# Three 64-column matmuls become one of 192 columns in the way back to edges of a graph layer

## The chip, the core and the metric

The kernel runs on one core of a Trainium2 chip. TensorE (PE) multiplies matrices and writes into PSUM, VectorE (DVE) and ScalarE (ACT) work element by element, GpSimd (POOL) here issues the gathers of rows from memory, and SyncE (SP) issues plain transfers. [...] The metric is the device time of one execution in microseconds (us). Three runs of the kernel before took 2152.33, 2159.18 and 2159.98 us; the median, 2159.18 us, is the time before.

## The reference

One layer of a graph network on 6250 nodes of 64 features and 206250 edges, the edges sorted by their target:

```python
def _L0_gnn_ref(x, edge_index, edge_attr, W1, b1, W2, b2):
    src = edge_index[0]
    dst = edge_index[1]
    msg = jax.nn.relu(x[src] + edge_attr)
    agg = jax.ops.segment_sum(msg, dst, num_segments=x.shape[0])
    h = x + agg
    h = jax.nn.relu(h @ W1 + b1)
    return h @ W2 + b2
...
h = jnp.maximum(_layernorm(x, axis=-1), 0.0)
x = x + _L0_gnn_ref(h, edge_index, edge_attr_64, L0_gnn_W1, L0_gnn_b1, L0_gnn_W2, L0_gnn_b2)
```

For every edge a row of the normed nodes is fetched (`x[src]`), the edge's attributes are added, a Relu is taken, and the messages are summed by target.

## The kernel before

**Groups and steps.** The edges are worked in 268 groups of 768 (`GE`), and a last part: 128 partitions times 6 columns (`G`), 64 features each. The function `half(g)` is one step of the main loop, for groups 5 to 268, so 264 steps. The order of all instructions is the order in which the program is written; the framework only places the semaphores, and each engine goes through its own instructions as fast as its waits allow.

**Two ways to fetch a row.** Of the 6 columns of a group the first three are gathered by POOL with indirect transfers, one for each column (`gather`, L175). The last three (`H` = 3) are fetched by TensorE with one-hot matrices, and this is the way that the change touches. The normed rows lie in SBUF as three bf16 parts side by side (`hp`, 3 x 64 = 192 columns), whose sum is the fp32 row. Two groups make a set `k`.

- `find` (VectorE, L394) compares node numbers and gives `found`, one-hot columns.
- `slots_of` (TensorE, L417) multiplies `found` with `hp`: 16 matmuls of 192 columns with 32 weights each for one u, two u to a PSUM tile `half`. `slots_out` (ScalarE, L425) casts a tile to bf16 in `picked`. In a step two such tiles come first, and two or one later.
- `back` (VectorE, L403) makes the one-hot matrices `backs`, 128x128, seven (`Q`) for each of the three columns.
- `pick(g, cols)` (TensorE, L434) takes the picked rows back to their edges: for each column u, each of 7 q and each of the 3 parts t one matmul of 64 columns, all 21 of a column accumulated into the same 64 columns of PSUM. A group has 63 such matmuls. Its result is the PSUM tile `pick`, of which there are two.

**What a step does, by engine.** TensorE in `half(g)`: the sum of the last group's messages by target, `window_sum(g-1)` (12 matmuls, L492); the first two tiles of `slots_of`; `pick(g+1, (0, 1))`; the later tiles of `slots_of`; `pick(g+1, (2,))`; in some steps matmuls for ranks and sources (L238, L240, L267, L279) and the dense layers (L509, L520). VectorE: `sum_into_z(g-2)` (L458) adds an older group's window to `z`; `messages(g)` adds gathered rows to the attributes `ea` (L478), and the picked ones (L480); then `one_hot` (L464), `back`, `find` and ranks. ScalarE: the casts of the first two tiles, the Relu of `messages(g)` (L482), the casts of the later tiles. POOL runs ahead: a gather waits only for a free buffer (`edge`, 12 of them), which VectorE's work on an older group sets free. SP loads attributes 9 groups ahead (`AHEAD`).

**PSUM.** [...] `rows` and `half` have two each; `pick` has two tiles; the windows of four groups (`AB` = 4) share a tile `agg`, and there are two of these. `window_sum(g-1)` comes before `sum_into_z(g-2)` in the program.

The lines around which the rest turns, in `half` and in `messages`:

```python
messages(g)
if g < NG:
    pick(g + 1, (0, 1))
...
nc.vector.tensor_tensor(ea[:, lo:m], ea[:, lo:m], xg[:, lo:m], ALU.add)
if m < G:
    nc.vector.tensor_tensor(ea[:, m:], ea[:, m:], picks.pop(g), ALU.add)
```

Of the kernel before, what the change touches and what calls it, by code (L numbers as in the profile page):

```python
# [9 lines left out]
F32 = mybir.dt.float32  # L10
# [5 lines left out]
ALU = mybir.AluOpType  # L16
AX = mybir.AxisListType
DVE = mybir.EngineType.DVE

N, E, D = 6250, 206250, 64  # L20
P = 128
G = 6
# [10 lines left out]
W = 32  # L33
# [5 lines left out]
LOOK = 12  # L39
AHEAD = 9  # L40
LAG = 2
AB = 4
RV = 16

H = 3
# [7 lines left out]
Q = PARTS * S // P  # L53
XC = 14
RAW = 5
F0 = RAW
# [13 lines left out]
def kernel(  # L70
# [14 lines left out]
    nc = tc.nc  # L85
# [7 lines left out]
    psum = ctx.enter_context(tc.tile_pool(name="psum", bufs=2, space=bass.MemoryType.PSUM))  # L93
# [85 lines left out]
    def first_col(g):  # L179
        return 0 if g < NG else G - CT  # L180

    def pool_cols(g):
        return G - H if g >= F0 else G
# [195 lines left out]
    backs, sources, spots, found, picked, halves, picks = {}, {}, {}, {}, {}, {}, {}  # L379

    def source_load(k):
        sources[k] = rank.tile([P, PARTS * 2 * S], I16, name="sources")
        nc.sync.dma_start(out=sources[k][:PP], in_=lines[k // SETS][k % SETS].rearrange("(o m) s -> o (m s)", o=1)
                          .to_broadcast([PP, PARTS * 2 * S]))

    def spot_load(k):
        spots[k] = rank.tile([P, 2 * H * P], BF16, name="spots")
        nc.sync.dma_start(out=spots[k], in_=spot_rows[k * 2 * H:(k + 1) * 2 * H, :]
                          .rearrange("(o t) s -> o (t s)", o=1).to_broadcast([P, 2 * H * P]))
# [9 lines left out]
    def back(k, q0, q1):  # L399
        if q0 == 0:  # L400
            backs[k] = hot.tile([P, Q, 2 * H, P], BF16, name="backs")
        for q in range(q0, q1):
            nc.vector.tensor_scalar(backs[k][:, q].rearrange("p t s -> p (t s)"), spots[k].bitcast(I16),  # L403
                                    ids[:, q:q + 1], None, op0=ALU.is_equal)
        if q1 == Q:
            spots.pop(k)
# [3 lines left out]
    def slots_of(k, n0):  # L410
        ps = psum.tile([P, 2, 3 * D], F32, name="half", bufs=2)
        for u in range(2):
            i, q = divmod(n0 + u, Q)
            for b in range(BB):
                for j in range(J):
                    m = q * J + j
                    nc.tensor.matmul(ps[j * S:(j + 1) * S, u], found[k][:PP, b, m, i, :],  # L417
                                     hp[:, b * PARTS + m].rearrange("p t d -> p (t d)"),
                                     start=(b == 0), stop=(b == BB - 1))
        if n0 == 0:  # L420
            picked[k] = hot.tile([P, 2 * Q, 3 * D], BF16, name="picked")
        halves[k, n0] = ps

    def slots_out(k, n0):
        nc.scalar.copy(picked[k][:, n0:n0 + 2], halves.pop((k, n0)))  # L425

    def pick(g, cols):
        k, i = divmod(g - F0, 2)
        if cols[0] == 0:
            picks[g] = psum.tile([P, H, D], F32, name="pick", bufs=2)  # L430
        for u in cols:
            for q in range(Q):
                for t in range(3):
                    nc.tensor.matmul(picks[g][:, u], backs[k][:, q, i * H + u, :],  # L434
                                     picked[k][:, i * Q + q, t * D:(t + 1) * D],
                                     start=(q == 0 and t == 0), stop=(q == Q - 1 and t == 2))

    def norm_edges(xg):
        s = work.tile([P, G], F32, name="raw_s")
        nc.vector.tensor_reduce(s, xg, AX.X, ALU.add)  # L440
        nc.vector.tensor_scalar_mul(s, s, 1.0 / D)
        nc.vector.tensor_tensor(xg, xg, s.unsqueeze(2).to_broadcast([P, G, D]), ALU.subtract)
        sq = work.tile([P, G, D], F32, name="msg", bufs=3)
        nc.scalar.activation(sq, xg, AF.Square)
        fill()
        v = work.tile([P, G], F32, name="raw_v")
        nc.vector.tensor_reduce(v, sq, AX.X, ALU.add)
        nc.scalar.activation(v, v, AF.Sqrt, bias=eps_sb, scale=1.0 / D)
        fill()
        nc.vector.reciprocal(v, v)  # L450
        nc.vector.scalar_tensor_tensor(xg, xg, 0.0, v.unsqueeze(2).to_broadcast([P, G, D]),
                                       op0=ALU.max, op1=ALU.mult)

    aggs, hots, taken, msgs, banks = {}, {}, {}, {}, []

    def sum_into_z(g):
        at = window_start(g)
        nc.vector.tensor_tensor(z[:, ds(at, W)], z[:, ds(at, W)], aggs.pop(g), ALU.add)  # L458

    def one_hot(g):  # L460
        lo = first_col(g)
        n = G - lo
        oh = work.tile([P, G, W], F32, name="oh")
        nc.vector.tensor_tensor(  # L464
            oh[:, lo:], slot[:, cols_of(g)].unsqueeze(2).to_broadcast([P, n, W]),
            slots[:, :W].unsqueeze(1).to_broadcast([P, n, W]), ALU.is_equal)
        hots[g] = oh

    def enter(g):
        if g <= NG and g not in taken:  # L470
            taken[g] = loaded[g] if g < RAW else load(g)

    def messages(g):
        lo, m = first_col(g), pool_cols(g)
        ea, xg = taken.pop(g)
        if g < RAW:
            norm_edges(xg)
        nc.vector.tensor_tensor(ea[:, lo:m], ea[:, lo:m], xg[:, lo:m], ALU.add)  # L478
        if m < G:
            nc.vector.tensor_tensor(ea[:, m:], ea[:, m:], picks.pop(g), ALU.add)  # L480
        msg = work.tile([P, G, D], F32, name="msg", bufs=3)
        nc.scalar.activation(msg[:, lo:], ea[:, lo:], AF.Relu)  # L482
        msgs[g] = msg

    def window_sum(g):
        lo, oh, msg = first_col(g), hots.pop(g), msgs.pop(g)
        if g % AB == 0:
            banks.append(psum.tile([P, AB, W], F32, name="agg", bufs=2))
        pa = banks[-1][:, g % AB]
        for j in range(lo, G):  # L490
            i = (j - lo) % 2
            nc.tensor.matmul(pa[i * D:(i + 1) * D], msg[:, j, :], oh[:, j, :], start=(j < lo + 2), stop=(j >= G - 2))  # L492
        aggs[g] = pa
# [41 lines left out]
    def blocks_behind(g):  # L535
        for c in sorted(res):
            store(c, *res.pop(c))
        for c in sorted(hid):
            res[c] = result(c, *hid.pop(c))
        for c in range(NB):  # L540
            if READY[c] == g:
                hid[c] = hidden(c)

    def chunk(i, then):

        if i % (2 * SETS) == 0 and 0 <= i // (2 * SETS) < NCH:
            then(i // (2 * SETS))

    def is_set(k):
        return 0 <= k < KS  # L550

    def half(g):
        k, i = divmod(g - F0, 2)
        first = ((0, 2), (8, 10))[i]
        later = ((4, 6), (12,))[i]
        now = is_set(k + 1)
        enter(g + AHEAD)
        if i == 0:
            if is_set(k + 3):
                source_load(k + 3)  # L560
        elif is_set(k + 3):
            spot_load(k + 3)
        if g >= 1:
            window_sum(g - 1)
        if now:
            for n0 in first:
                slots_of(k + 1, n0)
                slots_out(k + 1, n0)
        if g >= LAG:
            sum_into_z(g - LAG)  # L570
            blocks_behind(g - LAG)
        messages(g)
        if g < NG:
            pick(g + 1, (0, 1))
        if now:
            for n0 in later:
                slots_of(k + 1, n0)
                slots_out(k + 1, n0)
        if g < NG:
            pick(g + 1, (2,))  # L580
        one_hot(g)
        if i == 0:
            if is_set(k + 1):
                back(k + 1, 4, Q)
            if is_set(k + 2):
                find(k + 2, 0)
        else:
            if is_set(k + 2):
                back(k + 2, 0, 4)
                find(k + 2, 1)  # L590
        at = g - F0
        chunk(at + 14, rank_at)
        chunk(at + 13, rank_count)
        chunk(at + 12, rank_of)
        chunk(at + 11, rank_marks)
        chunk(at + 11, rank_turn)
        chunk(at + 10, rank_holds)
        chunk(at + 10, rank_fits)
        chunk(at + 9, source)
        if g in CHECKS:  # L600
            find_left(CHECKS.index(g))
# [90 lines left out]
        slots_out(0, n0)  # L692
    source_load(2)
    spot_load(2)
    pick(F0, (0, 1, 2))
    find(1, 0)
    find(1, 1)
    back(1, 0, 4)
# [25 lines left out]
    with tc.If(any_left > 0):  # L724
        with tc.For_i(0, NG, 1) as i:
# [4 lines left out]
            ea = edge.tile([P, G, D], F32, name="ea")  # L730
# [5 lines left out]
        ea = edge.tile([P, G, D], F32, name="ea")  # L736
# [46 lines left out]
```

## Time and profile before

| | |
|---|---|
| median of three runs | 2159.18 us |
| the profiled execution | 2166.87 us, of which the span of its instructions 2165.2 us |
| busy, TensorE matmuls | 1587.4 us (73%), 35792 matmuls |
| busy, weight loads | 1246.3 us (58%), 35792 |
| busy, VectorE | 964.1 us (45%) |
| busy, ScalarE | 598.1 us (28%) |
| busy, POOL | 864.5 us (40%) |
| granted TensorE clock, mean | 0.81 |

How to read the rows. A group of instructions by line reads: line, engine, operation, output<-input, shapes, count | busy us, mean ns of one | idle time of the engine before them and what ended it. A row of the time line reads: start (us from the span's start), duration, engine, line, operation, and in brackets the idle time before it. A row of windows reads: from:to, length, then for PE, PEld (weight loads), VectorE, ScalarE and POOL the busy time with the number of instructions in brackets, then the granted clock (1.00 is full), the share of the DMA engines in use and GB/s. "issue" is idle time for which the profile shows no wait. Matmuls overlap, so the duration of one is not its price; the distance from one group's start to the next one's is. A few per cent of the matmul records can be missing.

### The profile page before, as it was taken

How to read it: one execution, taken by the hardware profiler on the slowest of the kernel's cores; microseconds unless marked ns; L12 is line 12 of the kernel's file. 1: busy time of each engine (PE TensorE's matmuls, PEld its weight loads, DVE VectorE, ACT ScalarE, POOL GpSimd, SP SyncE). 2: the span in 40 equal slices, each digit the busy share in tenths (PEclk: the TensorE clock that was granted, in tenths of full speed). 3: DMA queues.
4: the chain of work that ended last, by engine and by line, in shares of the span. 5: the costliest groups of instructions: out<-in, count | busy, mean ns of one | idle time of the engine just before them, and what ended most of it. 6: DMA issues, size and time to landing. Idle time of an engine off the chain costs nothing.

```text
span 2165.2 us, 79562 instructions
## 1 busy us (share of the span) xinstructions
PE 1587.4 (73%) x35792; PEld 1246.3 (58%) x35792; DVE 964.1 (45%) x2721; ACT 598.1 (28%) x1351; POOL 864.5 (40%) x834
## 2 busy tenths in 40 slices
PE   1147787787778777777787778778777777778788
PEld 0135565565556655665565666556665566556566
DVE  7074443444444344444344444444444444444445
ACT  1132222232223222223222223222222322223223
POOL 7514433434444344434433443344434434443330
PEclk9998887777878788878778778777778987888779
DMA  5113233223333233333322323232323322323321
GB/s 165 29 47 88 73 95 81 71 75 83 78 81 88 80 74 77 88 79 88 83 72 76 88 72 90 75 85 74 89 71 82 96 76 70 89 77 91 81 77 35
DMA packets 112983, 172.67 MB, mean 80 GB/s; under 512 B 29185, under 2 KB 83585, under 8 KB 112637
## 3 DMA queue, kind: packets, MB, share of 16 engines
q1 hardware_dynamic: 85534, 139.02, 21.8%
q0 software_dynamic: 26240, 26.92, 7.5%
q8 instruction: 282, 4.62, 0.9%
q10 hardware_dynamic: 864, 1.60, 0.2%
q14 instruction: 63, 0.52, 0.1%
HBM read 163.56 MB, written 3.88 MB: 77 GB/s over the span
## 4 chain that ended last, share of the span: by engine, by line
PE 71%; issue 21%; another core or an unknown queue 3%; DVE 2%; DMA 2%; ACT 0%; DVEq 0%; POOL 0%; SPq 0%; ACTq 0%
PE pick L434 34%; PE half L417 25%; PE agg L492 8%; DMA x_sb<-in_x_dram 1%; PE rows L279 1%; PE rows L509 1%; PE rows L240 1%; PE rows L238 1%; PE rows L520 1%; PE rows L267 0%; DVE backs L403 0%; ACT z L318 0%; DVE found L394 0%; DVE rest L325 0%
## 5 line engine op out<-in xcount | busy, mean ns | idle before, releaser
L175 POOL DMA_INDIRECT xg<-h_rows,src_sb x790 | 831.1, 1052 | 1227.2 <-DVE ea L480 907.1
L434 PE MATMUL pick<-picked,backs 128*128 128x64 bf16 x16632 | 773.6, 207 | 245.3 <-issue 239.0
L434 PEld LDWEIGHTS <-backs 128*128 128x128 bf16 x16632 | 650.9, 107 | 412.4 <-issue 401.7
L425 ACT CAST picked<-half 128x384 bf16<-128x384 f32 x924 | 420.6, 480 | 1380.6 <-PE half L417 888.9
L417 PE MATMUL half<-hp,found 112*32 112x192 bf16 x14784 | 595.2, 283 | 196.9 <-issue 186.6
L417 PEld LDWEIGHTS <-found 112*32 112x32 bf16 x14784 | 379.6, 109 | 304.0 <-issue 267.7
L458 DVE TENSOR_TENSOR z<-z,agg 128x32 f32 x269 | 49.9, 185 | 714.1 <-PE agg L492 694.0
L403 DVE TENSOR_SCALAR backs<-spots,ids 128x768 bf16<-128x768 int16 x924 | 327.7, 414 | 0.0
L480 DVE TENSOR_TENSOR ea<-ea,pick 128x192 f32<-128x192 f32 x264 | 92.2, 349 | 407.7 <-PE pick L434 380.8
L492 PE MATMUL agg<-oh,msg 128*64 128x32 f32 x3224 | 187.9, 256 | 10.6 <-issue 8.1
L492 PEld LDWEIGHTS agg<-oh,msg 128*64 128x64 f32 x3224 | 153.2, 172 | 44.1 <-issue 27.8
L394 DVE TENSOR_SCALAR found<-sources,nodes_of 112x1792 bf16<-112x1792 int16 x264 | 178.0, 675 | 0.1
L482 ACT ACTIVATE msg<-ea 128x384 f32<-128x384 f32 x269 | 142.7, 530 | 5.3 <-DVE ea L478 3.0
L464 DVE TENSOR_TENSOR oh<-slot,slots 128x192 f32<-128x192 int16 x269 | 94.4, 351 | 0.0
L478 DVE TENSOR_TENSOR ea<-ea,xg 128x192 f32<-128x192 f32 x264 | 93.6, 355 | 0.7
L317 PE MATMUL rows<-ident,x_sb 112*64 112x112 f32 x56 | 12.7, 394 | 49.9 <-issue 42.5
L238 PE MATMUL rows<-at,upper 128*128 128x504 bf16 x44 | 25.7, 585 | 22.8 <-DVE at L232 21.5
L317 PEld LDWEIGHTS rows<-ident,x_sb 112*64 112x64 f32 x56 | 7.7, 160 | 55.2 <-issue 45.9
L279 PE MATMUL rows<-holds,marks 128*28 128x32 bf16 x792 | 29.5, 185 | 11.3 <-DVE holds L257 5.9
L175 POOL DMA_INDIRECT xr<-in_x_dram,src_sb x30 | 31.1, 1035 | 10.6 <-issue 8.8
L279 PEld LDWEIGHTS <-marks 128*28 128x28 bf16 x792 | 24.2, 100 | 15.5 <-DVE holds L257 6.0
L257 DVE TENSOR_TENSOR holds<-rank_of,from 128x576 bf16<-128x576 f32 x44 | 32.9, 749 | 0.0
(94 smaller groups left out, 391.3 us busy)
## 6 DMA issues: line engine op xcount, KB each, us to landing
sources<-source_row SPq DMA_DIRECT2D x132, 392.0 KB
ea<-in_edge_attr_dram SPq DMA_DIRECT2D x268, 192.0 KB
spots<-spot_rows SPq DMA_DIRECT2D x132, 192.0 KB
xg<-h_rows,src_sb POOLq DMA_INDIRECT x790
h_rows<-x_sb SPq DMA_DIRECT2D x4, 392.0 KB
x_sb<-in_x_dram SPq DMA_DIRECT2D x4, 388.5 KB
xb<-in_x_dram SPq DMA_DIRECT2D x12, 128.0 KB
out_dram<-o SPq DMA_DIRECT2D x12, 128.0 KB
```

The costliest lines, as they stand in the source:

```text
L175: nc.gpsimd.indirect_dma_start(out=xg[:, j, :], out_offset=None, in_=rows[:, :], in_offset=bass.IndirectOffsetOnAxis(ap=idx[:, j:j + 1], a ...
L279: nc.tensor.matmul(ps[:, i], mk[:, i * H + t, :], oh[:, i * H + t, :], start=(t == 0), stop=(t == H - 1))
L394: nc.vector.tensor_scalar(found[k][:PP, b].rearrange("p m i s -> p (m i s)"), sources[k][:PP], nodes_of[:PP, b:b + 1], None, op0=ALU.is_equal)
L403: nc.vector.tensor_scalar(backs[k][:, q].rearrange("p t s -> p (t s)"), spots[k].bitcast(I16), ids[:, q:q + 1], None, op0=ALU.is_equal)
L417: nc.tensor.matmul(ps[j * S:(j + 1) * S, u], found[k][:PP, b, m, i, :], hp[:, b * PARTS + m].rearrange("p t d -> p (t d)"), start=(b == 0) ...
L425: nc.scalar.copy(picked[k][:, n0:n0 + 2], halves.pop((k, n0)))
L434: nc.tensor.matmul(picks[g][:, u], backs[k][:, q, i * H + u, :], picked[k][:, i * Q + q, t * D:(t + 1) * D], start=(q == 0 and t == 0), st ...
L464: nc.vector.tensor_tensor(oh[:, lo:], slot[:, cols_of(g)].unsqueeze(2).to_broadcast([P, n, W]), slots[:, :W].unsqueeze(1).to_broadcast([P, ...
L478: nc.vector.tensor_tensor(ea[:, lo:m], ea[:, lo:m], xg[:, lo:m], ALU.add)
L480: nc.vector.tensor_tensor(ea[:, m:], ea[:, m:], picks.pop(g), ALU.add)
L482: nc.scalar.activation(msg[:, lo:], ea[:, lo:], AF.Relu)
L492: nc.tensor.matmul(pa[i * D:(i + 1) * D], msg[:, j, :], oh[:, j, :], start=(j < lo + 2), stop=(j >= G - 2))
```

## The change

`pick` writes all three parts with one matmul: 192 columns of `picked` go into 192 columns of PSUM, and only the 7 q are accumulated. A group then has 21 matmuls in place of 63, and the sum over the parts is left to VectorE. A new function `room` takes two PSUM tiles for a group, of two columns and of one, each column with four parts of 64; ScalarE copies the edges' attributes into the fourth part. In `messages` VectorE sums the four parts with a `tensor_reduce` for each tile and writes the result over the attributes, in place of the addition at L480. `room(g + 1)` stands in `half` between `messages(g)` and `pick(g + 1, (0, 1))`. [...]

```diff
-AB = 4
+AB = 8
...
     def pick(g, cols):
         k, i = divmod(g - F0, 2)
-        if cols[0] == 0:
-            picks[g] = psum.tile([P, H, D], F32, name="pick", bufs=2)
+        ps, lo = picks[g][len(picks[g]) - 2 + (cols[0] > 0)]
         for u in cols:
             for q in range(Q):
-                for t in range(3):
-                    nc.tensor.matmul(picks[g][:, u], backs[k][:, q, i * H + u, :],
-                                     picked[k][:, i * Q + q, t * D:(t + 1) * D],
-                                     start=(q == 0 and t == 0), stop=(q == Q - 1 and t == 2))
+                nc.tensor.matmul(ps[:, u - lo, :3].rearrange("p t d -> p (t d)"), backs[k][:, q, i * H + u, :],
+                                 picked[k][:, i * Q + q], start=(q == 0), stop=(q == Q - 1))
+
+    def room(g):
+        ea, m = taken[g][0], G - H
+        picks[g] = []
+        for lo, n in ((0, 2), (2, 1)):
+            ps = psum.tile([P, 2, 4, D], F32, name="pick", bufs=3)
+            nc.scalar.copy(ps[:, :n, 3], ea[:, m + lo:m + lo + n])
+            picks[g].append((ps, lo))
...
-    aggs, hots, taken, msgs, banks = {}, {}, {}, {}, []
+    aggs, hots, taken, msgs = {}, {}, {}, {}
+    bank = psum.tile([P, AB, W], F32, name="agg", bufs=1)
...
         if m < G:
-            nc.vector.tensor_tensor(ea[:, m:], ea[:, m:], picks.pop(g), ALU.add)
+            for (ps, at), n in zip(picks.pop(g), (2, 1)):
+                nc.vector.tensor_reduce(ea[:, m + at:m + at + n], ps[:, :n].rearrange("p j t d -> p j d t"), AX.X, ALU.add)
...
     def window_sum(g):
         lo, oh, msg = first_col(g), hots.pop(g), msgs.pop(g)
-        if g % AB == 0:
-            banks.append(psum.tile([P, AB, W], F32, name="agg", bufs=2))
-        pa = banks[-1][:, g % AB]
+        pa = bank[:, g % AB]
...
         messages(g)
         if g < NG:
+            room(g + 1)
             pick(g + 1, (0, 1))
...
-    pick(F0, (0, 1, 2))
+    room(F0)
+    pick(F0, (0, 1))
+    pick(F0, (2,))
```

## The prediction

> **What bounds the kernel now.** I read the page's chain of waits first, then its groups by line, the time line of one step, and last the busy times in short windows. A "step" below is one call of `half`, one group of 768 edges.
>
> ```profile
> PE 71%; issue 21%; another core or an unknown queue 3%; DVE 2%; DMA 2%; ACT 0%; DVEq 0%; POOL 0%; SPq 0%; ACTq 0%
> PE pick L434 34%; PE half L417 25%; PE agg L492 8%; DMA x_sb<-in_x_dram 1%; PE rows L279 1%; PE rows L509 1%; PE rows L240 1%; PE rows L238 1%; PE rows L520 1%; PE rows L267 0%; DVE backs L403 0%; ACT z L318 0%; DVE found L394 0%; DVE rest L325 0%
> L434 PE MATMUL pick<-picked,backs 128*128 128x64 bf16 x16632 | 773.6, 207 | 245.3 <-issue 239.0
> 143.30:2155.70 2012.40, 1557.55 (x35499) 1226.92 (x35494) 888.84 (x2575) 565.41 (x1288) 795.94 (x754) 0.80 0.31 80
> ```
>
> TensorE sets the end: 71% work, 21% "issue", where it waits for no semaphore. The main loop (last row) is 2012.4 us for 264 steps, 7.62 us each, at a mean clock of 0.80. The issue time has a place. These are windows over three batches of gathers on POOL, each split where TensorE's first long gap begins; the counts in brackets after the first two busy times are its matmuls and weight loads.
>
> ```profile
> 1010.08:1011.44 1.36, 1.31 (x47) 1.05 (x43) 1.36 (x5) 0.70 (x2) 1.08 (x1) 1.00 0.04 12
> 1011.44:1018.02 6.58, 2.36 (x33) 1.35 (x34) 1.18 (x4) 0.00 (x0) 4.80 (x5) 0.84 0.14 25
> 1026.06:1027.46 1.40, 1.26 (x40) 1.15 (x41) 1.40 (x5) 0.99 (x3) 1.09 (x2) 1.00 0.06 15
> 1027.46:1030.39 2.93, 1.40 (x19) 0.55 (x18) 0.78 (x2) 0.00 (x0) 1.95 (x2) 0.85 0.46 80
> 1228.68:1231.06 2.38, 2.38 (x55) 2.07 (x48) 2.38 (x7) 1.35 (x3) 2.07 (x2) 0.53 0.09 14
> 1231.06:1235.89 4.83, 1.68 (x26) 0.83 (x22) 0.76 (x3) 0.00 (x0) 3.61 (x5) 0.84 0.16 30
> ```
>
> While POOL gathers, TensorE gets some 80 to 100 instructions, at either clock, and then only 10 to 13 per us (67 in 6.58 us, 37 in 2.93, 48 in 4.83) until shortly after the batch. I read this as a reserve that is used up while the supply nearly stops; the reserve is an inference from the equal counts. A batch of three holds this for 4.33 us (1.40 + 2.93) and lets 118 instructions pass. So the number of instructions counts, more than their columns.
>
> **The price of columns.** Windows from one group's start to the next one's, then a time line:
>
> ```profile
> 1053.21:1055.56 2.35, 2.35 (x46) 2.26 (x42) 0.68 (x2) 0.92 (x3) 0.00 (x0) 0.50 0.91 250
> 1024.01:1024.73 0.72, 0.72 (x25) 0.67 (x21) 0.00 (x0) 0.66 (x2) 0.00 (x0) 1.00 0.98 188
> 1009.59:1010.92 1.33, 1.33 (x46) 1.28 (x43) 1.33 (x6) 1.19 (x3) 0.84 (x1) 1.00 0.14 25
> 1023.24:1024.01 0.77, 0.77 (x35) 0.61 (x32) 0.00 (x0) 0.20 (x1) 0.00 (x0) 1.00 0.91 302
> ...
> 1019.10 0.86 PE L492 MATMUL agg<-oh,msg 128*64 128x32 f32 x12
> 1019.89 1.47 PE L417 MATMUL half<-hp,found 112*32 112x192 bf16 x32
> 1021.29 2.02 PE L434 MATMUL pick<-picked,backs 128*128 128x64 bf16 x42
> ```
>
> At full clock 42 matmuls of 64 columns take 1.33 us and 21 take 0.72: 29 ns each and 0.11 fixed. At half clock 2.35 us for 42 is 53 ns each. For a 192-column matmul against 128 weights there is no row; the ends are 83 ns (32 matmuls of 192 columns at L417, four side by side, 0.77 us less 0.11, over 8) and 3 x 29 = 87. I take 83, and at half clock 3 x 53 = 160. So one matmul for three saves hardly any streaming: pick of two columns goes from 1.33 to 14 x 0.083 + 0.11 = 1.27 us, of the third from 0.72 to 0.69; at half clock both stay (2.35, 1.23). What it removes is 42 matmuls and 42 weight loads of about 270 instructions a step.
>
> **The wait that it adds.** `room` puts ScalarE copies ahead of pick, into the same PSUM tile. Whether a matmul then waits, though its columns are others, I read from the sums:
>
> ```profile
> 1024.73 0.54 PE L492 MATMUL agg<-oh,msg 128*64 128x32 f32 x12
> 1025.20 0.84 PE L417 MATMUL half<-hp,found 112*32 112x192 bf16 x32
> 1025.32 0.19 DVE L458 TENSOR_TENSOR z<-z,agg 128x32 f32 x1 [3.56 <-PE agg L492]
> 1025.43 0.36 DVE L478 TENSOR_TENSOR ea<-ea,xg 128x192 f32<-128x192 f32 x1
> 1025.71 0.35 DVE L480 TENSOR_TENSOR ea<-ea,pick 128x192 f32<-128x192 f32 x1
> 1025.77 0.86 ACT L425 CAST picked<-half 128x384 bf16<-128x384 f32 x2 [1.10 <-PE half L417]
> 1025.97 0.35 DVE L464 TENSOR_TENSOR oh<-slot,slots 128x192 f32<-128x192 int16 x1
> 1026.06 1.08 POOL L175 DMA_INDIRECT xg<-h_rows,src_sb  x1 [8.58 <-DVE ea L480]
> 1026.52 0.54 ACT L482 ACTIVATE msg<-ea 128x384 f32<-128x384 f32 x1
> ...
> 1012.18 0.18 DVE L458 TENSOR_TENSOR z<-z,agg 128x32 f32 x1
> ```
>
> L458 reads the window of an older group, yet it starts 0.05 us after the matmuls of the newest window end (1025.27): two engines on different columns of one PSUM tile are put in order. In the step at 1012.18 it doesn't wait; there the two windows lie in different tiles. With one `bank` of eight, VectorE waits in every step. I take it that pick waits for its copy likewise. On ScalarE that copy stands behind two casts and the Relu, and the Relu behind VectorE's sums. [...]
>
> ```profile
> L440 DVE TENSOR_REDUCE raw_s<-xr 128x6 f32<-128x384 f32 x5 | 2.7, 547 | 0.1
> L289 DVE TENSOR_REDUCE ln_s<-x_sb 112x14 f32<-112x896 f32 x4 | 4.3, 1086 | 4.6 <-DMA x_sb<-in_x_dram 4.6
> L318 ACT COPY z<-rows 64x448 f32<-64x448 f32 x12 | 6.4, 542 | 49.2 <-remote 42.1 <-PE rows L616 4.2 <-PE rows L317 1.9
> L318 ACT COPY z<-rows 64x224 f32<-64x224 f32 x4 | 1.4, 357 | 9.4 <-remote 9.4
> ```
>
> A reduce costs 1.05 ns an element and 0.14 us (539 ns for 512 more), so 512 elements 0.68 us and 256 0.41, against 0.35 for L480. These read the four parts with a stride, which no row shows; the low end is these prices less a tenth, the high end twice them. A copy is 0.83 ns a column and 0.17 us: 0.28 and 0.23.
>
> From the window's end (1025.20 is zero) at full clock: first reduce 0.51, second 1.10 (an operation's successor starts 0.09 before its end), end 1.51; Relu 1.56; copy 2.00 to 2.28 (Relu 0.53, overlap 0.09); pick 2.32. It now starts at 0.77, so TensorE stands 1.55 us in each step. At half clock the casts hold the Relu until 1.88 (the second block ends at 1.40), pick starts at 2.65: 1.25 us. Queued behind pick on TensorE is the rest of the step. The second copy ends before pick's third column is due. VectorE's added 0.74 us a step (195 us in all) and ScalarE's 0.5 lie beside TensorE: they have 889 and 565 us of work in the loop's 2012; only what stands in this chain counts. POOL's gathers go by L478 or L480 (ends 1025.79, 1026.06; the batch at 1010.08 runs on into a second one before the next L480), so I leave their start at 0.86.
>
> **The sum for a step.** Full clock before: first block 0.77; the batch from 0.86 to 5.19 lets 118 instructions pass, pick's 81 and 37 of the later block's 48 (64 or 32); 0.14 for those left, 0.72, some 0.40 for ranks and dense layers (an estimate), 0.47 for the window: 6.9 us. Half clock: 0.54 us of the first block (25), pick's 84 and 14 of the later block pass by 5.19; 0.75 + 1.23 + 0.50 + 0.79 follow: 8.46. With full clock for 60% of the time, which gives 0.80: 1/(0.6/6.9 + 0.4/8.46) = 7.45, against 7.62 measured.
>
> After, full clock: 0.77 + 1.55 + 1.27 + 0.61 + 0.69 + 0.40 + 0.47 = 5.75; only some 105 instructions fall in the batch, fewer than the 118 it lets pass, so the starving is gone. Half clock: 1.40 + 1.25 + 2.35 + 1.08 + 1.23 + 0.50 + 0.79 = 8.60. The clock goes with how busy the window before was:
>
> ```profile
> 1009.04:1012.46 3.42, 2.71 (x72) 1.95 (x71) 3.12 (x11) 1.28 (x3) 2.08 (x2) 1.00 0.13 24
> 1012.46:1015.87 3.41, 1.09 (x20) 0.69 (x18) 0.16 (x1) 0.00 (x0) 2.50 (x4) 1.00 0.15 28
> 1015.87:1019.28 3.41, 1.27 (x24) 1.04 (x26) 0.32 (x2) 0.52 (x2) 1.31 (x2) 0.50 0.12 20
> 1026.11:1029.52 3.41, 2.11 (x50) 1.51 (x49) 2.13 (x6) 0.94 (x3) 2.80 (x3) 1.00 0.26 28
> 1029.52:1032.94 3.42, 3.04 (x36) 1.84 (x37) 0.00 (x0) 0.48 (x1) 0.20 (x1) 0.50 0.58 182
> ```
>
> A window busy for 2.71 of 3.42 us is followed by full clock, those with 1.09 and 2.11 by half. A window that holds the whole stall is busy for about 1.9, so I take half the time at each clock: 1/(0.5/5.75 + 0.5/8.60) = 6.89, 0.56 us less than 7.45. [...] Over 264 steps 0.56 us is 147 us: 2166.87 for the profiled execution (span 2165.2) becomes 2020; the median of the runs lies 8 lower, so 2012.
>
> **The rivals.**
> No reserve after the stall (slower): what passes in a batch doesn't wait in a buffer, so pick resumes in the starved stretch at 12.6 instructions per us. From 2.32 to 5.19 pass 36, the remaining 40 and the rest take 2.06: 7.25 at full clock, with 8.60 mixed 7.87, +0.42 a step: 2269. It decides where fewer than about 60 instructions pass at once after the wait. Against it stand the equal counts at both clocks.
> A dear reduce: at twice its price the stall grows by 1.0 us, 6.75 and 9.6 give 7.93: 2285. From 0.55 us more the change loses. For it: four elements to a sum, strided. Against it: VectorE's rows all go by elements.
> The clock drops further, to 30% at full: 7.49, no change, 2169. For it: stall and remaining gaps are apart, so more windows have one. Against it: the starving, which drops it now, shrinks.
> No wait for the copies, if the two are told apart by columns: no stall, starving late in the step, 5.5 and 7.35 at 60%: 6.12, which is 1808. Against it stands L458.
>
> **How the numbers follow.** Forecast 0.57, no reserve 0.14, dear reduce 0.10, lower clock 0.12, no wait 0.07. The forecast alone spans 1925 to 2100 (share of full clock 60% to 40%, cheap or slightly dearer reduces). Down to 1925 and up to 2250 some 0.79 lie inside, with the lower clock and the lower part of the slow cases. Runs differ by 0.35% (2152.33 to 2159.98), so within 0.5% counts as the same. Faster: forecast and no wait, 0.64, and 0.03 of the clock case; same 0.06; slower 0.14 + 0.10 + 0.03.
>
> **What would show it.** Right: TensorE idle before L434's successor by some 1.5 us a step, released by ScalarE's copy; "issue" time down by more than half; gathers in batches of three only; reduces at 0.68 and 0.41 us. Wrong: pick following its block without a gap; gaps of 0.7 us right behind the stall; reduces above 1 us; a loop clock under 0.7.

## The result: 1803 us, and the profile after

| | before | after |
|---|---|---|
| median of four runs each, same chip | 2159.58 us | 1803.39 us (1787.49 to 1814.54) |
| ratio | | 0.833, 95% interval 0.827 to 0.839 |
| profiled execution, of which span | 2166.87, 2165.2 us | 1814.54, 1812.8 us |
| mean granted clock over the span | 0.81 | 0.92 |
| TensorE matmuls | 35792 | 24704 |
| VectorE busy | 964.1 us | 1137.3 us |

The change saves 356 us; 147 were forecast, and 1803 lies below the predicted range. All numbers of this section are from the chip of this comparison; other chips behave differently, which is shown further down. The profiled execution after is the slowest of its four, at a mean clock of 0.92 where the other three show 0.93 to 0.94.

The page's chain of waits can't be read this time: for the changed kernel it breaks off after some per cent of the span. The waits of TensorE are the first view instead. The columns are: waiting engine and line, what ended the wait, total us, times, longest us.

```profile
PE pick L432 <- ACT pick L440: 380.6, 244, 4.1
PE pick L432 <- issue: 17.1, 41, 3.3
```

The wait for ScalarE's copy is there, 380.6 us or 1.44 us a step (over 264 steps; the shares of a few steps are booked elsewhere). "Issue" ahead of `pick` fell from 239.0 to 17.1 us. Next are the page's line of the clock in 40 slices and its groups; last the groups kept apart by shape.

```profile
PEclk9999998998989989998999899889898899999889
L432 PE MATMUL pick<-picked,backs 128*128 128x192 bf16 x5544 | 635.1, 268 | 427.2 <-ACT pick L440 380.6
L417 PE MATMUL half<-hp,found 112*32 112x192 bf16 x14784 | 438.0, 260 | 9.9 <-DVE found L394 5.3
```

```profile
L487 DVE TENSOR_REDUCE ea<-pick 128x128 f32<-128x512 f32 x264 | 180.5, 684 | 0.1
L487 DVE TENSOR_REDUCE ea<-pick 128x64 f32<-128x256 f32 x264 | 109.5, 415 | 0.0
L440 ACT COPY pick<-ea 128x128 f32<-128x128 f32 x264 | 69.0, 261 | 0.0
L440 ACT COPY pick<-ea 128x64 f32<-128x64 f32 x264 | 54.1, 205 | 0.0
```

At L417, where the kernel before lost 186.6 us to "issue", TensorE now idles for 9.9 us in all. The reduces and copies cost what was forecast (0.684 and 0.415 us against 0.68 and 0.41; 0.261 and 0.205 against 0.28 and 0.23).

One step at full clock in the time line:

```profile
1003.65 0.54 PE L497 MATMUL agg<-oh,msg 128*64 128x32 f32 x12
1004.12 0.84 PE L417 MATMUL half<-hp,found 112*32 112x192 bf16 x32
1004.24 0.19 DVE L464 TENSOR_TENSOR z<-z,agg 128x32 f32 x1 [3.63 <-PE agg L497]
1004.41 0.36 DVE L484 TENSOR_TENSOR ea<-ea,xg 128x192 f32<-128x192 f32 x1
1004.69 1.01 DVE L487 TENSOR_REDUCE ea<-pick 128x128 f32<-128x512 f32 x2
1005.04 0.95 POOL L175 DMA_INDIRECT xg<-h_rows,src_sb  x1 [3.62 <-DVE ea L484]
1005.74 0.52 ACT L489 ACTIVATE msg<-ea 128x384 f32<-128x384 f32 x1 [0.20 <-DVE ea L487]
1006.17 0.40 ACT L440 COPY pick<-ea 128x128 f32<-128x128 f32 x2
1006.48 1.31 PE L432 MATMUL pick<-picked,backs 128*128 128x192 bf16 x14 [1.52 <-ACT pick L440]
1007.73 0.84 PE L417 MATMUL half<-hp,found 112*32 112x192 bf16 x32
1008.50 0.75 PE L432 MATMUL pick<-picked,backs 128*128 128x192 bf16 x7
```

The chain runs window, sum into `z`, addition, reduces, Relu, copy, `pick`, as it was worked out. The gathers start at 1005.04, and TensorE stands until 1006.48; then 14, 32 and 7 matmuls follow without a gap while POOL still gathers. From 1006.48 to 1007.73 the 14 matmuls take 1.25 us. All batches of gathers but two after the first 200 us have three: 243 of 245. Before, 123 had three, 58 six and 2 nine, where gathers less than 0.6 us apart count as one batch.

The whole loop, from the first `pick` to the last, in the view of windows:

```profile
143.14:1802.59 1659.45, 1224.02 (x24406) 987.05 (x24406) 1061.26 (x2837) 648.65 (x1814) 828.51 (x754) 0.92 0.35 96
```

That is 6.29 us a step against 7.62, with the clock at 0.92 against 0.80. The records of the clock in these two loops hold two values only, 1 and 0.5; half clock ruled for 816 of 2012 us before (41%) and for 276 of 1659 us after (17%). Idle time moved from "issue" to the copy and hardly shrank: 455 us in the loop before, of which `pick` and `half` lost 425.6 to "issue", and 435 after. What fell is work at half clock: TensorE was busy there for 659 us before and 255 after, and at full clock for 899 and 969. Its busy time in the loop went from 1557.55 to 1224.02 us, though 21 matmuls of 192 columns stream as many columns as 63 of 64.

### The profile page after: what moved, and what is told of

Read it like the earlier page. It is cut to its first block, busy times and chain, and to the rows that moved or that the text cites. A ratio compares the mean times of both kernels' runs of the same rounds, so it can differ in the third digit from the quotient of the medians.

```text
span 1812.8 us, 57727 instructions
## 1 busy us (share of the span) xinstructions
PE 1254.3 (69%) x24704; PEld 1006.5 (56%) x24704; DVE 1137.3 (63%) x2985; ACT 682.1 (38%) x1879; POOL 897.7 (50%) x834
## 3 DMA queue, kind: packets, MB, share of 16 engines
q0 software_dynamic: 26240, 26.92, 8.0%
## 5 line engine op out<-in xcount | busy, mean ns | idle before, releaser
L175 POOL DMA_INDIRECT xg<-h_rows,src_sb x790 | 863.7, 1093 | 826.4 <-DVE ea L484 651.4
L432 PE MATMUL pick<-picked,backs 128*128 128x192 bf16 x5544 | 635.1, 268 | 427.2 <-ACT pick L440 380.6
L432 PEld LDWEIGHTS <-backs 128*128 128x128 bf16 x5544 | 510.9, 106 | 537.4 <-issue 523.9
L425 ACT CAST picked<-half 128x384 bf16<-128x384 f32 x924 | 410.9, 481 | 918.5 <-PE half L417 827.6
L417 PE MATMUL half<-hp,found 112*32 112x192 bf16 x14784 | 438.0, 260 | 9.9 <-DVE found L394 5.3
L417 PEld LDWEIGHTS <-found 112*32 112x32 bf16 x14784 | 308.4, 100 | 74.5 <-issue 52.5
L487 DVE TENSOR_REDUCE ea<-pick 128x128 f32<-128x512 f32 (+1 forms) x528 | 268.1, 549 | 0.1
L497 PE MATMUL agg<-oh,msg 128*64 128x32 f32 x3224 | 156.6, 230 | 4.7 <-DVE z L464 1.1
L497 PEld LDWEIGHTS agg<-oh,msg 128*64 128x64 f32 x3224 | 126.3, 141 | 45.1 <-issue 33.5
L440 ACT COPY pick<-ea 128x128 f32<-128x128 f32 (+1 forms) x528 | 105.7, 233 | 0.0
```

The source lines that it names most:

```text
L175: nc.gpsimd.indirect_dma_start(out=xg[:, j, :], out_offset=None, in_=rows[:, :], in_offset=bass.IndirectOffsetOnAxis(ap=idx[:, j:j + 1], a ...
L432: nc.tensor.matmul(ps[:, u - lo, :3].rearrange("p t d -> p (t d)"), backs[k][:, q, i * H + u, :], picked[k][:, i * Q + q], start=(q == 0), ...
L440: nc.scalar.copy(ps[:, :n, 3], ea[:, m + lo:m + lo + n])
L487: nc.vector.tensor_reduce(ea[:, m + at:m + at + n], ps[:, :n].rearrange("p j t d -> p j d t"), AX.X, ALU.add)
```

## The experiments

"To starve" here means that TensorE idles for "issue" while POOL gathers. In the next three groups the chips do so, as the one above does: the kernel before took 2122.83 us beside e1 to e4 and 2128.98 us beside e5 to e8. The kernel after was not run beside them; where a run is set against it, it is the one above, on a chip where the kernel before is 1.4 to 1.7% slower.

### What each part is worth

**e4_one_bank.** Against the kernel before; the windows of eight groups in one tile that stays, nothing else.

```diff
-AB = 4
+AB = 8
+    bank = psum.tile([P, AB, W], F32, name="agg", bufs=1)
...
-        if g % AB == 0:
-            banks.append(psum.tile([P, AB, W], F32, name="agg", bufs=2))
-        pa = banks[-1][:, g % AB]
+        pa = bank[:, g % AB]
```

> The kernel before with the one lasting tile of eight windows alone. Theory 1 (VectorE now waits in every step, and the double batches of gathers fall apart into batches of three, each with a reserve of its own): 0 to 60 us less, 2100 to 2160 us. Theory 2 (the added wait of VectorE in every fourth step delays what follows): 2170 to 2220 us.

Measured: 1908.07 us, ratio 0.898 (0.891 to 0.906), more than the first theory allowed. Its waits, and its loop in windows:

```profile
PE half L417 <- issue: 158.2, 411, 0.5
PE pick L434 <- issue: 130.0, 333, 1.3
```

```profile
131.70:1892.99 1761.29, 1450.09 (x35499) 1144.85 (x35495) 893.31 (x2574) 566.06 (x1288) 850.74 (x754) 0.88 0.33 91
```

"Issue" ahead of these two lines falls from 425.6 to 288.2 us, the clock rises to 0.88, and 237 of 240 batches have three gathers. So this part of the edit, which makes VectorE wait in each step for the newest window, gains 10% by itself.

**e2_three_matmuls.** Against the kernel after; the 63 matmuls of 64 columns come back, with the four parts, copies and reduces kept.

```diff
-            for q in range(Q):
-                nc.tensor.matmul(ps[:, u - lo, :3].rearrange("p t d -> p (t d)"), backs[k][:, q, i * H + u, :],
-                                 picked[k][:, i * Q + q], start=(q == 0), stop=(q == Q - 1))
+            for t in range(3):
+                for q in range(Q):
+                    nc.tensor.matmul(ps[:, u - lo, t], backs[k][:, q, i * H + u, :],
+                                     picked[k][:, i * Q + q, t * D:(t + 1) * D], start=(q == 0), stop=(q == Q - 1))
```

> The changed kernel with the copies, the four parts, the reduces and the one bank kept, but three matmuls of 64 columns, one for each part, in place of one of 192: 63 matmuls and weight loads a group again. Theory 1 (the number of instructions passes too slowly beside the gathers): the starving is back on top of the stall, issue time over 250 us, 2100 to 2200 us. Theory 2 (the gain comes from the columns or from the sums on VectorE): only 0.09 us a step of streaming is lost, 1820 to 1840 us.

Measured: 1992.5 us, ratio 0.939 (0.933 to 0.944), between the theories, nearer to the first, whose 250 us of "issue" were not reached either. Its waits:

```profile
PE pick L433 <- ACT pick L441: 370.3, 242, 3.1
PE half L417 <- issue: 135.3, 351, 0.5
```

The stall is the same as after, and behind it the matmuls starve again: 135.3 us at L417, where all idle time together is 9.9 us with 21 matmuls. The columns streamed are equal in both kernels. So the number of instructions counts: with 21 matmuls the same kernel takes 1803 us.

**e1_early_copy.** Against the kernel after; the copy for the first two columns is written at the start of the step, ahead of the casts and the Relu, the other stays.

```diff
+        if g < NG:
+            room(g + 1, ((0, 2),))
         if now:
...
         if g < NG:
-            room(g + 1)
+            room(g + 1, ((2, 1),))
             pick(g + 1, (0, 1))
```

> The changed kernel, with the first copy of room (two columns) moved to the start of the step, ahead of the casts; the second stays behind the Relu. Theory 1 (the stall covers starving): TensorE's stall of 1.44 us a step (380.6 us in all) goes, but its instructions then meet the gathers earlier, run through their reserve of some 80 and starve; a step at full clock only falls from 5.75 to about 5.5: 1720 to 1770 us. Theory 2 (the stall lies on the path and nothing takes its place): 380 us less, 1420 to 1460 us.

Measured: 1632.58 us, ratio 0.766 (0.760 to 0.772), between the theories. Its waits:

```profile
PE pick L432 <- ACT pick L440: 18.7, 22, 2.7
PE half L417 <- issue: 56.0, 149, 0.5
PE agg L497 <- issue: 48.6, 153, 0.5
PE pick L432 <- issue: 28.5, 101, 0.5
```

380.6 us of stall become 18.7, which shows that the copy's place made the stall. Some 133 us of "issue" come back in the last three rows: without the stall more instructions fall into a batch. That is why the whole stall wasn't gained.

On these chips, one part laid on the other, the ratio goes 1, 0.898 (one bank), 0.939 (parts, reduces and the copy's wait), 0.833 (21 matmuls for 63; another chip), 0.766 (earlier copy). The order matters, since each part changes what the next one meets. The new matmuls beside the old windows were not run: with two tiles for `rows`, two for `half`, three for `pick` and two for `agg` that kernel has nine, where the kernels before and after have eight each.

### Are the gathers the cause

**e3_plain_rows** and **e8_plain_pool** against the kernel before, **e5_after_plain** against the kernel after: for all groups past the first five, fixed rows are fetched by plain transfers of the same size in place of the rows named by the indices, by SyncE in e3 and e5, by POOL in e8.

```diff
-        gather(xg[:, lo:], src_sb[:, g * G + lo:g * G + hi], hi - lo, x if g < RAW else h_rows)
+        if g < RAW:
+            gather(xg[:, lo:], src_sb[:, g * G + lo:g * G + hi], hi - lo, x)
+        else:
+            for j in range(hi - lo):
+                nc.sync.dma_start(out=xg[:, lo + j, :], in_=h_rows[j * P:(j + 1) * P, :])
```

> The kernel before, with POOL's indirect gathers of the main loop replaced by plain transfers of 128 consecutive rows, issued by SyncE (so the messages of these columns are of other nodes). Theory 1 (POOL's gathers hold up TensorE's instructions): issue time falls from 430 us to under 100, 1700 to 1800 us. Theory 2 (TensorE is held up by its own volume of instructions, the gathers only run at the same time): issue time stays over 350 us, 2120 to 2170 us.

> The kernel before with plain transfers of 128 consecutive rows as in e3, but issued by POOL. Theory 1a (what holds TensorE up is POOL making descriptors from indices): as e3, 1300 to 1450 us. Theory 1b (any transfer that POOL issues does it): 1850 us or more.

> The changed kernel with the plain transfers of e3 in place of POOL's gathers. Theory 1 (without gathers nothing starves, so the stall behind the copies comes out in full and fewer matmuls save only their streaming, 0.09 us a step): e3's 1313 us and 264 times 1.44 less 0.09, about 1670 us: the change makes this kernel slower. Theory 2 (fewer instructions save time at any rate): 1200 to 1320 us.

Measured: e3 1312.79 us (ratio 0.617, 0.613 to 0.621), far more than the first theory's gain; e8 1345.77 us, within its theory 1a; e5 1638.57 us, near the 1670 of its first theory. The waits of e3, of e5, and POOL's group on the page of e8:

```profile
PE pick L438 <- issue: 29.6, 32, 2.0
PE half L421 <- issue: 28.6, 30, 2.1
```

```profile
PE pick L436 <- ACT pick L444: 397.4, 264, 4.4
```

```profile
L197 POOL DMA_DIRECT2D xg<-h_rows x790 | 537.9, 687 | 706.7 <-DVE ea L484 618.2 <-DVE ea L482 63.4 <-issue 11.3
```

Without indirect gathers the starving is gone and with it 38% of the time. With as many transfers, 790, and as many bytes, 26.92 MB, from POOL's queue it is gone too, so neither POOL's queue nor the bytes are the cause, but something that comes with the indirect form. Which part of it is open, and the descriptors of theory 1a are not shown by any row: the plain transfers also read the same consecutive rows for every group, and keep POOL busy for 687 ns each in place of 1052. Indirect gathers of fixed rows were not run. And where there is no starving, the change makes the kernel slower: e3 takes 1313 us, e5, on another chip, 1639 (beside e8's 1346). The stall of 397.4 us is then a plain loss.

### Two tests of the other way

**e6_two_windows.** Against the kernel before: `AB = 2` in place of 4, so that two windows share a tile.

> The kernel before with two windows to a tile (AB = 2) in place of four, two tiles. Theory 1 (in each step whose two windows lie in different tiles VectorE runs ahead and the gathers come in a batch of six, which starves TensorE for longer on one reserve): every other step does so, some 130 batches of six in place of 58; e4 has 3 and is 215 us faster, 3.9 us for each, so 2300 to 2450 us. Theory 2 (e4's gain came from the single bank, not from the order of the gathers): 2100 to 2150 us.

Measured: 2341.2 us (the kernel before 2128.98), inside the first theory's range; clock 0.74. POOL's time line and TensorE's wait:

```profile
1015.56 1.08 POOL L175 DMA_INDIRECT xg<-h_rows,src_sb  x1 [9.90 <-DVE ea L480]
1016.94 1.01 POOL L175 DMA_INDIRECT xg<-h_rows,src_sb  x1 [0.30 <-issue]
1018.26 0.95 POOL L175 DMA_INDIRECT xg<-h_rows,src_sb  x1 [0.30 <-issue]
1019.51 0.94 POOL L175 DMA_INDIRECT xg<-h_rows,src_sb  x1 [0.30 <-issue]
```

```profile
PE pick L434 <- issue: 365.2, 631, 1.4
```

Gathers now come in sixes, 117 of 127 batches, after 9.9 us of rest (the last two lie past these rows), and "issue" ahead of `pick` grows from 239.0 to 365.2 us. Same instructions, same gathers: the batch's length is what changed. With four windows to a tile VectorE's sum waits for the newest window 191 times, with two 133 times, with the one lasting tile 240 times. So e4 and e6 agree that sharing a PSUM tile sets in which step VectorE waits, and that this sets how many gathers POOL has in a row; e16 below doesn't fit as well.

**e7_long_stall.** Against the kernel after: the first copy is made six times.

```diff
-            nc.scalar.copy(ps[:, :n, 3], ea[:, m + lo:m + lo + n])
+            for _ in range(6 if n == 2 else 1):
+                nc.scalar.copy(ps[:, :n, 3], ea[:, m + lo:m + lo + n])
```

> The changed kernel with the first copy of room made six times, 0.9 us more in the chain of each step. Theory 1 (the clock goes by the time that TensorE streams in a window of 3.41 us, and drops below some 0.45 of it): a window with a stall of 2.35 us streams for 0.31, the mean clock falls to about 0.8 and the time rises by more than the stall, to 2080 to 2180 us. Theory 2 (the clock doesn't mind stalls of this length): clock 0.92 as before, 264 times 0.9, about 2040 us or less.

Measured: 2374.34 us, above both theories. The five more copies took 1.51 us (1.91 for the row below, 0.40 in the time line above), not 0.9. Its time line and wait:

```profile
1004.35 1.91 ACT L441 COPY pick<-ea 128x128 f32<-128x128 f32 x7
1006.16 1.31 PE L432 MATMUL pick<-picked,backs 128*128 128x192 bf16 x14 [2.95 <-ACT pick L441]
```

```profile
PE pick L432 <- ACT pick L441: 810.2, 264, 5.0
```

The wait goes from 1.44 to 3.07 us a step and the clock from 0.92 to 0.82. The step grew from 6.29 to 8.44 us, 0.52 more than the 1.63 of the wait; the lower clock goes with it. So this longer stall did cost clock, as the first theory had it.

### Spacing the gathers, and other chips

To spread the batches out, **spread_before** puts a fill of a spare row (1 x 320) on POOL behind each gather; **spread_early** does so in e1's kernel. **one_window** is the kernel before with `AB = 1`. They were first sent to a chip on which the kernel before took 1343.13 us, then to another at 1353.0, and last to one at 2117.32.

```diff
+            if pad is not None:
+                nc.gpsimd.memset(pad, 0.0)
```

> The kernel before with one window to a tile (AB = 1), two tiles: VectorE's sum never lies in the tile that TensorE writes, so it waits for no newer window in any step. Theory 1 (what costs is that batches of gathers meet, whatever keeps them apart): with the wait gone from every step, VectorE is held by pick alone, once a step, the batches stay at three, and the time is near e4's, 1880 to 1980 us. Theory 2 (only the wait for the window keeps VectorE from running ahead): batches of six or more, 2120 us or more.

> The kernel before with a small fill of a spare row on POOL behind each gather of the main loop, some 0.35 us each, so that the gathers of a batch stand further apart. Theory 1 (a gather stops the supply of TensorE's instructions while POOL works on it, and a reserve of some 64 to 80 fills again in the gap): issue time is halved at least, 1600 to 1850 us. Theory 2 (what counts is the time that gathers take in all): 2090 us or more.

> e1 (the changed kernel with the first copy at the start of the step) with the fills of e10. Theory 1: what is left of the starving goes as well, 1480 to 1600 us against 1633. Theory 2: 1630 us or more.

Measured: ratios 1.000 (0.996 to 1.004), 1.004 (1.001 to 1.008) and 1.015 (1.010 to 1.020). They decide nothing on what they were made for: 19 runs of the kernel before lay between 1334 and 1359 us, as fast as without indirect gathers above. The same program, unchanged, is 37% shorter on this chip. That made the next question whether the change is any good there.

> The changed kernel itself, unaltered. On the chip of e9 to e11 the kernel before took 1343 us, as little as without gathers (e3, e8), so there gathers don't hold TensorE up. Theory 1 (the gain is only what TensorE lost to gathers, and the stall of 1.44 us a step is always paid): where the kernel before takes some 1340 us, this takes 1620 to 1680 us, as e5; where it takes some 2130 us, 1770 to 1820. Theory 2 (fewer instructions gain on any chip): below the kernel before on both.

> The kernel of e9 again (AB = 1), for a chip on which gathers hold TensorE up. If the kernel before takes some 2130 us: theory 1 (batches kept apart by anything) 1880 to 1980 us, theory 2 (only the wait for the window keeps them apart) 2120 or more. If it takes some 1340 us: no difference, as e9.

> The kernel of e10 again, for a chip on which gathers hold TensorE up. If the kernel before takes some 2130 us: theory 1 (a reserve that refills in the gaps) 1600 to 1850 us, theory 2 (only the gathers' total time counts) 2090 or more. If it takes some 1340 us: no difference, as e10.

> The kernel of e1 again. If the kernel before takes some 2130 us: 1600 to 1650 as e1. If it takes some 1340 us: theory 1 (without starving and without the stall only the streaming is saved, and VectorE has 195 us more) 1300 to 1370 us; theory 2 (fewer instructions still gain) under 1280 us.

Measured beside a kernel before of 1353.0 us: e12, the changed kernel itself, 1661.89 us, ratio 1.234 (1.220 to 1.247), slower as its first theory says. e13 1.000 (0.995 to 1.005), e14 1.006 (1.001 to 1.010). e15, the early copy, 1249.8 us, ratio 0.927 (0.917 to 0.936), as its second theory says. Waits and loop of e12; then the same of e13, which runs in the time of the kernel before and stands for it, with its POOL row; then e15's:

```profile
PE pick L432 <- ACT pick L440: 402.3, 264, 4.5
```

```profile
94.78:1644.34 1549.56, 1146.36 (x24406) 938.66 (x24406) 1060.87 (x2837) 655.08 (x1814) 831.14 (x760) 0.95 0.37 103
```

```profile
PE pick L434 <- issue: 52.8, 45, 2.4
PE half L417 <- issue: 28.1, 28, 2.6
```

```profile
94.05:1324.62 1230.57, 1133.61 (x35498) 969.67 (x35495) 894.29 (x2577) 551.74 (x1289) 802.44 (x760) 0.99 0.49 131
```

```profile
L175 POOL DMA_INDIRECT xg<-h_rows,src_sb x790 | 841.0, 1065 | 387.9 <-issue 202.9
```

```profile
PE pick L432 <- ACT pick L440: 46.3, 57, 4.5
```

On this chip the gathers do not starve TensorE: 80.9 us of "issue" at the two lines, against 425.6, with gathers of the same length (1065 ns against 1052). Steps are 1549.56 / 264 = 5.87 us after and 4.66 before. The difference, 1.21 us, equals the stall (402.3 / 264 = 1.52) less the issue time that is gone (80.9 / 264 = 0.31). With the stall mostly removed (46.3 us in e15) the edit still gains 7%. How much of that comes from fewer instructions and how much from its other parts is not shown: they were not run apart on such a chip.

Back on a chip that starves, one round each, so the intervals are wide:

> The kernel of e9 and e13 again, should the chip be one where the kernel before takes some 2130 us. Theory 1 (batches of gathers kept apart by anything): 1880 to 1980 us. Theory 2 (only the wait for the window keeps them apart): 2120 us or more. Where the kernel before takes some 1350 us: no difference.

> The kernel of e10 and e14 again, should the chip be one where the kernel before takes some 2130 us. Theory 1 (a reserve of instructions that refills in the gaps between gathers): 1600 to 1850 us. Theory 2 (only the gathers' total time counts): 2090 us or more. Where the kernel before takes some 1350 us: no difference.

> The kernel of e11 again, should the chip be one where the kernel before takes some 2130 us. Theory 1: what is left of e1's starving goes as well, 1480 to 1600 us against e1's 1633. Theory 2: 1630 us or more. Where the kernel before takes some 1350 us: some 1365 us, as e11, with POOL as the bound.

Measured: e16 2082.33 us, ratio 0.989 (0.950 to 1.028); e17 1991.16, 0.946 (0.918 to 0.973); both between their theories. e18 1541.91, 0.732 (0.715 to 0.750), as its first theory says. In e16 VectorE's sum waits for a window for less than 168.9 us in all, against 694.0 in the kernel before, but its addition waits for `pick`, 595.6 us; 170 batches have three gathers and 33 six, yet the time isn't e4's. So the length of the batches alone doesn't give the time, and with two runs each this stays open.

Spacing helps where the gathers starve: e17 against the kernel before, and e18 with 0.732 against e1's 0.766, on different chips. Where they don't, it costs 0.4 to 0.6% in the kernel before (e10, e14) and takes away the whole gain of the early copy: e11 has 1.015 where e15 has 0.927, again on different chips. POOL's rows in e11 show why:

```profile
L177 POOL DMA_INDIRECT xg<-h_rows,src_sb x790 | 824.7, 1044 | 132.9 <-issue 116.6
L181 POOL MEMSET spare<- 1x320 f32 x790 | 343.5, 435 | 0.0
```

With the fills POOL is at work for 1168 of 1358 us and idle ahead of the gathers for 133, so POOL itself seems to set the pace. The early copy (e1, e15) beats both kernels on both kinds of chip; e18 is the best where gathers starve, e15 where they don't.

## Why the prediction was right in sign and short by 209 us

**Right, by its own steps.** The wait of `pick` for its copy: 1.44 us a step, where 1.55 and 1.25 stood. Its cause: e1 takes the wait away, e7 lengthens it. The prices of matmuls (1.25 us for 14, where 1.27 stood), reduces and copies. The end of the starving, and its reason, fewer instructions in a batch: e2 brings 135 us of it back. The step at full clock: 5.75 and 8.60, mixed by e12's clock (0.95, so 10% at half), give 1 / (0.90/5.75 + 0.10/8.60) = 5.95, against 5.87 measured.

**The step that failed** is "A window that holds the whole stall is busy for about 1.9, so I take half the time at each clock". Measured were 17% at half clock, not 50%. With 83% of the time at full the same prices give 1 / (0.83/5.75 + 0.17/8.60) = 6.09, not 6.89. These 0.80 us over 264 steps are 211 us, and 209 were missing. What is left nearly cancels: 6.29 measured against 6.09, and a base of 7.45 against 7.62. Two things were wrong in it. These windows of the changed kernel lie on the grid of the clock's records, which begin and end in steps of 3.41 us; after the length stand busy time and matmuls, and the clock is third from the end:

```profile
995.78:999.20 3.42, 1.89 (x51) 1.35 (x49) 2.19 (x7) 2.48 (x7) 1.15 (x2) 1.00 0.21 59
999.20:1002.61 3.41, 3.41 (x33) 2.67 (x33) 1.40 (x4) 0.28 (x2) 1.91 (x2) 0.50 0.15 29
...
1009.44:1012.85 3.41, 1.75 (x49) 1.55 (x50) 2.85 (x9) 2.55 (x7) 1.74 (x2) 1.00 0.35 101
1012.85:1016.27 3.42, 3.42 (x35) 2.65 (x34) 0.81 (x2) 0.48 (x1) 1.31 (x2) 0.50 0.32 115
1016.27:1019.68 3.41, 1.92 (x50) 1.42 (x48) 2.22 (x7) 1.58 (x5) 1.11 (x2) 1.00 0.29 87
1019.68:1023.09 3.41, 3.39 (x65) 2.88 (x65) 2.54 (x6) 0.52 (x3) 2.16 (x2) 1.00 0.32 85
```

First, the threshold. Windows busy for 1.89 and 1.75 us are followed by half clock, one busy for 1.92 by full. The row that set the threshold in the prediction (2.11, then half) came from a starved stretch, where each matmul counts as busy for the length of its record, 207 ns in the mean at L434, though the next one can start 29 ns behind it. Counted by the distance from matmul to matmul (the way of counting is in the last section), that row streams for 1.47 us and the three here for 1.37, 1.42 and 1.52: all but the last are followed by half. Over the whole loop 132 windows at full clock hold a whole wait of `pick` for its copy, and only 37 of them are followed by half; the other 29 of 66 falls come behind windows that hold none. Second, not every window holds one: a stall of 1.55 us in a step of 5.75 lies whole within (3.41 - 1.55) / 5.75 = 32% of windows. Even if each of these had cost one window at half clock, the share would have been 0.32 / 1.32 = 24%, the step 6.25 and the forecast 2012 - 264 x (6.89 - 6.25) = 1843 us. The number was there to be worked out, and a guess of one half took its place.

**The base of the sum.** "A batch of three" was used for the kernel before, and the sixes were mentioned only in passing. e4 has threes alone, and its step is 1761.29 / 264 = 6.67 us; the sum's 6.9 and 8.46 at e4's clock (0.88, 76% at full) give 7.22. So a step with batches of three was priced 0.55 us too high and the sixes were left out; the two errors nearly met at 7.45, beside 7.62 measured. That a sum meets the time before is no proof of its terms. The edit to one bank had no term of its own; alone it is worth 10%.

**The rivals.** No reserve after the stall falls with the time line: 53 matmuls follow the stall in a batch without a gap. A dear reduce falls with 0.684 and 0.415 us. A lower clock falls: it rose to 0.92; that it can fall, e7 shows. The time of "no wait" (1808) was met, but its mechanism wasn't: the wait is there in full. The sign, too, holds only for a chip whose gathers starve TensorE. No step of the prediction doubted that, and a trace from one chip can't show it.

## What to carry to other kernels

Before an idle cause is priced, find out on how many chips it exists: here the same edit is 17% faster on one chip and 23% slower on another, and the version that is faster on both comes from moving one copy ahead of the work it doesn't need. In the kernel after, the copy into the PSUM tile stands behind two casts and the Relu on ScalarE; issued ahead of them, in e1, it left 18.7 us of the 380.6 that `pick` waited. And where a clock has two states, count the windows that would fall and multiply; one share guessed by eye cost this forecast more than all its other terms.

## What the runs showed of the hardware

- **The gathers' effect differed from chip to chip.** On chips of four comparisons the kernel before took 2094 to 2161 us, on two others 1334 to 1369. Each chip was seen in one comparison only, so whether this belongs to the chip or to the moment isn't shown. A gather is as long on both kinds (1052 ns in the kernel before, 1065 in e13). That it is the supply of instructions that fails is inferred from "issue" time and from the counts of instructions: within the batches of the kernel before, 9 matmuls and weight loads pass between two gaps of over 0.25 us (median), and such a spell repeats every 0.75 us. The pages also list transfers of instructions on a queue of their own (q8), of 16 KiB each: 282 in the kernel before and 195 in the kernel after. That they bring TensorE's is an estimate from their number: 71584 matmuls and weight loads before and 49408 after make 254 and 253 for each. They take 1.10 us inside the batches of the kernel before and 1.07 outside (medians); and in the loop of the kernel before 278 of them stand against 1305 such gaps. So in this run the starving isn't these transfers taking longer. Why chips differ, and what an indirect gather does that a plain transfer from the same queue does not, stays open.
- **In these two loops the clock fell behind windows that were far from idle.** Each matmul was counted by its distance to the next one, but at most 29 ns (at half clock 53) for 64 columns and 25 ns more. Of the windows of 3.41 us at full clock that were filled by this for less than 40%, none of 99 is followed by full clock in the loop before and 1 of 29 in the loop after; at 40 to 50% it is 19 of 35 and 90 of 128; above 50% it is all of them. Of the windows at half clock 10 of 41 and 4 of 11 that were filled for 70 to 80% are followed by full clock, and 100 of 101 and 62 of 62 above that. With another way of counting these bounds move. The way back asked for more here, so that a fall cost more than one window now and then: in the loop after, 66 falls led to 81 windows at half.
- **The sum over four parts with a stride cost no more than one over neighbours:** 0.684 us for 512 elements from PSUM and 0.415 for 256 (L487), 1.05 ns for each further element, as in the reduces of the kernel before (539 ns for 512 more).
